# Router logits from rows less their mean, the inverse root applied behind the product, the last tile's comparisons on VectorE, and a pair's absorbed weights made inside the last tile's chain

## The chip, the cores and the metric

The kernel runs on one core of a Trainium2 chip. The metric is device time in microseconds (us) from launch to end on the slowest core, of which there is one here; lower is better. A kernel is timed in several runs and the median is taken. Names of engines: PE is the matmul engine (TensorE), DVE is VectorE, ACT is ScalarE, POOL is GpSimd and SP is SyncE, which issues most of the DMAs.

## The reference

The input x is 16 x 56 tokens of 256 numbers; a context of 16 x 1500 keys of 64 numbers stays the same in all layers. There are four layers of gated cross attention, each followed by a gated feed-forward part:

```python
x = x + jnp.tanh(g_xattn[l]) * attention_l(_layernorm(x, axis=-1), ctx_512, ...)
x = x + jnp.tanh(g_ffn[l])   * ffn_l(_layernorm(x, axis=-1), ...)
```

Layer 0 is plain attention with 16 heads and a mixture of 16 experts (the best 4 for each token) with a shared expert. Layers 1 to 3 are latent attention: a head's scores are a product of a turned query and the context, `scores = einsum('bhsr,bhlr->bhsl', q_r, k_r)`, a softmax over the keys, a weighted sum of the context and an output product. The feed-forward parts concerned here are those of layers 2 and 3:

```python
# layer 2: 8 experts, the best one
route = jax.nn.sigmoid(x @ router_w)
max_ind = jnp.argmax(route, axis=1)
# layer 3: 16 experts, the best four, weights divided by their sum
logits = jnp.einsum('bsh,eh->bse', x, router_w) + expert_bias
scores = jax.nn.softmax(logits, axis=-1)
top_w, top_idx = jax.lax.top_k(scores, TOP_K)
```

In both, x is the normalised row: `(x - m) / jnp.sqrt(v + eps)`. The factor 1/sqrt(v + eps) is one number for each row, so it can be applied to a row before the product with the router's weights, or to the row of logits behind it.

## The kernel before

**Tiles and stages.** x lies in the core's memory as 8 tiles of 112 tokens. The weights of latent attention are absorbed: for each of 8 pairs of heads, `absorbing` (L242 to L299) multiplies weights with weights in four stages, each some matmuls and one copy from PSUM: e (L274, L278), f (L282, L284), M (L291, L293) and G (L298, L299). `Next.absorb(...)` runs these stages for pairs of the layer that comes next. `queries(l)` (L314 on) makes all queries of the layer by pairs (L331, M times the normalised rows); pairs that are not ready yet are made inside it. Absorbed pairs that are ready come from the expert stage before.

**Attention.** `attention_mla` (L642 to L860) does 56 steps in a layer: 8 tiles by 7 groups of 128 query rows. The order on every engine is written out by hand: `in_order` pins each instruction in the order of the program text. The loop runs over k and works on three steps at once: step k gets its scores (L703) with the maxima of its first half (L715, L717), its exponentials (L726, L735), the maxima of its second half (L720) and `invert` (L746, L747: two sums of the denominators on POOL; L748: the reciprocal on DVE; L750: a transpose on DVE; then DMAs on SP that spread it). Step k-1 gets its probabilities turned (L765, with copies on DVE at L768 for two of the six groups and on ACT at L770 for four; the groups 1 to 3 go through the banks in which step k's first half had its scores). Step k-2 gets the product with the values (L777) and its scaling on DVE (L788).

**The router's chain.** After the last step of a tile, `project(t)` becomes the generator `after`: the output product (L800) and the addition to x (L802), then `router.token_tile(t)` (L921 to L1022). The loop advances it three yields a step:

```python
                next(after, None)
                if new:
                    new.exps0()
                    new.maxima1()
                next(after, None)
                next(after, None)
```

So the number of yields between two parts of `token_tile` sets how many steps apart they come, and the place of each on its engine's queue. The parts are: mean and variance (L928, L929); the inverse root, by shifts and three Newton rounds on DVE (L131 to L141, three yields behind the first round); the normalised row xr (L932); copies of xr for the four experts, two on ACT and one on POOL (L938), in layer 3 alone; transposes (L941) and their copy (L943); logits (L949); softmax or sigmoid (L954 to L971); comparisons of all pairs of experts (L977, L978 on DVE, L979, L980 on POOL); ranks (L984, L986); the counting product (L990, L992); places (L996 to L1010); and the scatter of each row to its experts' places in DRAM, an indirect DMA on POOL for each (L1013: four in layer 3, one in layer 2).

**The seam to the experts.** Behind the last step `attention_mla` drains `after` for the last tile. Then `moe` (L1165 on) makes the table of tiles (`r.table()`, L1117 on), runs `occupy(n)` (L115 to L119: n matmuls of ones in bf16 whose result nobody reads) and walks over tiles of 128 rows: row load (L1204), weight loads (L1197, L1198), transposes (L1211, L1213), gate and up products (L1223), activation (L1227, L1228), transposes of the hidden rows (L1234), down product (L1245) and the store of results (L1248). In layer 2 the absorbed pair 0 of layer 3 is made between `occupy` and the tiles, the pairs 1 and 2 behind them, and the weights of pair 2 are loaded when tile 3 is at work (L1306).

Of the kernel before, what the change touches and what calls it, by code (L numbers as in the profile page):

```python
# [41 lines left out]
ALU = mybir.AluOpType  # L42
# [3 lines left out]
B, S, D = 16, 56, 256  # L46
# [3 lines left out]
NT = B // 2  # L50
# [24 lines left out]
def flamingo_kernel(ctx: ExitStack, tc: tile.TileContext, d: dict, out: bass.AP):  # L75
    nc = tc.nc
# [38 lines left out]
    def occupy(n):  # L115

        ps = misc()
        for _ in range(n):
            in_order(nc.tensor.matmul(ps, onesb[:, 0:128], onesb, start=True, stop=True))  # L119
# [26 lines left out]
        return y  # L146

    def inverse_root_now(pool, var, n):
        root = inverse_root(pool, var, n)
        while True:  # L150
            try:
                next(root)
            except StopIteration as e:
                return e.value
# [37 lines left out]
    class Next:  # L192
# [11 lines left out]
        def absorb(self, *gs):  # L204

            todo = [absorbing(self.l, g, self.G, self.pool, self.made, in_order) for g in gs]
            while todo:
                todo = [a for a in todo if next(a, self) is not self]

        def tile(self, t):  # L210

# [24 lines left out]
    def load_absorbed(l, g):  # L236
        loaded[l, g] = [
            load_heads(n, d[f"L{l}_{n}"], g)
            for n in ("wqr", "wkr", "wkc", "wq", "wkv", "wo")
        ]  # L240
# [401 lines left out]
    def attention_mla(l, nxt, router=None, behind=None, tail=None):  # L642

        with ExitStack() as st:
# [173 lines left out]
            for k in range(n + 2):  # L818
# [30 lines left out]
                if val and val.j == nq - 1:  # L849
                    for _ in after:  # L850
                        pass
                    after = project(val.t)
            if tail is None:
                for _ in after:
                    pass
            else:

                next(after)
                next(after)
            return after  # L860


# [39 lines left out]
    class Router:  # L902
# [18 lines left out]
        def token_tile(self, t):  # L921
# [5 lines left out]
            mv = pool.tile([TP, 2], F32, name="mv")  # L927
            in_order(nc.vector.bn_stats(st, x[:, t, :]))  # L928
            in_order(nc.vector.bn_aggr(mv, st))  # L929
            rstd = yield from inverse_root(pool, mv[:, 1:2])  # L930
            xr = pool.tile([TP, top, DX], F32, name="xr")
            in_order(nc.vector.tensor_scalar(xr[:, 0, 0:D], x[:, t, :], mv[:, 0:1], rstd, ALU.subtract, ALU.mult))  # L932
            yield
            c = C_D4 + 4 * t if top == 4 else C_D1 + t
            in_order(nc.gpsimd.tensor_copy(xr[:, :, D : D + 1], small[0:TP, c : c + top].unsqueeze(2)))
            for j in range(1, top):
                copy = nc.gpsimd.tensor_copy if j == 3 else nc.scalar.copy
                in_order(copy(xr[:, j, 0:D], xr[:, 0, 0:D]))  # L938
            ps = misc()
            for k in range(2):  # L940
                in_order(nc.tensor.transpose(ps[:, k * TP : (k + 1) * TP], xr[:, 0, k * 128 : (k + 1) * 128], ident[0:TP, 0:TP]))  # L941
# [1 line left out]
            in_order(nc.scalar.copy(xt, ps[:, 0 : 2 * TP].rearrange("p (k c) -> p k c", k=2)))  # L943
            yield
            yield
            yield
            lg = misc()[0:TP, 0:n_e]
            for k in range(2):
                in_order(nc.tensor.matmul(lg, xt[:, k, :], self.wr[:, k, :], start=k == 0, stop=k == 1))  # L949
            p = pool.tile([TP, n_e], F32, name="p")  # L950
            red = pool.tile([TP, 2], F32, name="red")
            yield
            if l == 2:
                in_order(nc.vector.tensor_copy(p, lg))  # L954
            else:
                in_order(nc.vector.tensor_tensor(p, lg, self.bias, ALU.add))
                in_order(nc.vector.tensor_reduce(red[:, 0:1], p, AX.X, ALU.max, negate=True))
            yield
            yield
# [16 lines left out]
            rank = pool.tile([TP, n_e], F32, name="rank")  # L976
            in_order(nc.vector.tensor_tensor(eq, others, mine, ALU.is_equal))  # L977
            in_order(nc.vector.tensor_tensor(gt, others, mine, ALU.is_gt))  # L978
            in_order(nc.gpsimd.tensor_tensor(eq, eq, tri[:, 0:n_e, 0:n_e], ALU.mult))  # L979
            in_order(nc.gpsimd.tensor_tensor(gt, gt, eq, ALU.add))  # L980
            yield
            yield
            yield
# [178 lines left out]
            in_order(nc.sync.dma_start(rows[e * CT : (e + 1) * CT].rearrange("c p x -> p c x"), bcast(zero, 1, CT)))  # L1162
            yield

    def moe(r, nxt=None, tail=None, rest=None):  # L1165

        l = r.l
        n_e, ft, nf, top, n_t, n_sure = MOE[l]
# [2 lines left out]
        with ExitStack() as st:  # L1171
# [85 lines left out]
            if l == 0:  # L1257


                sh = Shared(pool, ps_h, ps_o, side)  # L1260
                now = [part for e in range(2) for part in sh.parts(e, 0)]
                between = [part for e in range(2) for part in sh.parts(e, 1)]
                before, last = tail
                next(last)
                now[0][0]()
                next(before)
                next(last)
                next(last)
                next(before)
                next(last)  # L1270
                next(last)
                now[1][0]()
                next(last)
                r.table()
                next(last)
                next(last)
                next(last)
            else:
                r.table()
            by_pe = {0: (0, 1, 3, 4, 5, 6), 2: (), 3: (0, 2, 4, 5, 6)}[l]  # L1280
            diag = {}
# [21 lines left out]

            def during(i):
                if l == 2 and i == 3:
                    load_absorbed(3, 2)  # L1306
                if i % 3 == 0 and rest:
                    next(rest, None)
                if i % 4 == 3 and between:
# [23 lines left out]
            else:  # L1333
                pd = pool("d", 1)
                r.finish_weights()
                occupy(14 if l == 3 else 8)
                if l == 2:
                    nxt.absorb(0)
            tiles(0, n_sure, weights, loads, during)
            for _ in rest or ():  # L1340
                pass
# [1 line left out]
            with tc.If(live > n_sure):  # L1343
                tiles(n_sure, n_t, [], [])
            if nxt:
                nxt.absorb(*((0, 1) if l == 0 else (1, 2)))
            right.close()
            pt = pool("t", NT, **side)
            back = []
# [213 lines left out]
        for _ in left:  # L1563
            pass
    with routed(2) as r:
        attention_mla(2, nxt, r)
        nxt.whole.close()
        nxt = Next(3)
        moe(r, nxt)
    with routed(3) as r:  # L1570
        attention_mla(3, nxt, r)
        nxt.whole.close()
        moe(r)

# [142 lines left out]
```

## Time and profile before

| | us |
|---|---|
| median of 3 runs | 2395.82 |
| the runs | 2396.52, 2392.44, 2395.82 |
| profiled execution, its own time | 2395.73 |
| its span | 2393.6 |

The span runs from the first to the last instruction; what lies around it is 2.1 us. The clock that PE was granted is 0.964 of full speed over the span.

| engine | busy us | share of the span |
|---|---|---|
| PE | 2244.0 | 94% |
| DVE | 1531.0 | 64% |
| ACT | 1231.9 | 51% |
| POOL | 411.6 | 17% |

Where the groups of the table of costs are shown, a line reads: line of the kernel, engine, operation, output and inputs with their shapes, and the count, then busy time, the mean of one in nanoseconds, and the idle time of that engine just before them with what ended most of it. Two lines for the parts that the steps of attention are made of:

```profile
L703 PE MATMUL s_ps<-kvT,qT 64*128 64x500 f32 x2016 | 485.0, 608 | 11.2 <-ACT p L735 4.6
L777 PE MATMUL m_ps<-pT,kv 125*64 125x128 f32 x8064 | 477.3, 275 | 1.8 <-ACT pT L770 1.2
```

A timeline line gives the start in us from the span's start, the length, the engine, the line and the operation; in brackets stands how long the engine was idle before it and what released it. In the list of waits a line says who waited for whom, then the total in us, how many times, and the longest.

The stretches that matter are layer 2's attention (its first score group behind the first projection of that layer at 1249.16, and its last work near 1565), the seam behind it (the expert loop's first gate product at 1585.22), layer 3's queries (from about 1655), layer 3's attention (to about 2224) and the seam behind that (first gate product at 2244.53).

### The profile page before, as it was taken

The numbers are of one execution on the slowest core, as the hardware profiler recorded it, in microseconds if no ns is written. First come the engines' busy times: TensorE is split into PE (matmuls) and PEld (weight loads), VectorE is DVE, ScalarE is ACT, GpSimd is POOL, SyncE is SP. The second block draws the span as 40 slices with busy tenths as digits, with TensorE's granted clock in tenths as the row PEclk, the third lists the DMA queues.
The fourth block names the chain that finished last, engine by engine and source line by source line (L and its number), as shares of the span: only waits on it lengthen the run. The fifth ranks groups of instructions, "written<-read, shape, count | busy, mean of one in ns | idle before, by whom it ended". The sixth has DMA issues, their size and how long they took to land. (4 is left out here: it accounts for less than half of the span.)

```text
span 2393.6 us, 47915 instructions
## 1 busy us (share of the span) xinstructions
PE 2244.0 (94%) x17842; PEld 1611.7 (67%) x17842; DVE 1531.0 (64%) x3552; ACT 1231.9 (51%) x2703; POOL 411.6 (17%) x707
## 2 busy tenths in 40 slices
PE   8678989999999999999999999979899999999697
PEld 5445655777777776447777777745577777777454
DVE  5752245778777777667777777724577777776222
ACT  4312336666666663346666666513566666665131
POOL 5454710000000002420000000001001111111233
PEclk9769989999999999989999999999899999999899
DMA  7726752000000002100000000054101000000597
GB/s 226 217 87 190 228 140 81 22 21 22 21 21 22 21 23 69 54 28 21 24 24 11 23 22 23 11 209 148 34 22 30 29 20 26 26 26 18 158 285 205
DMA packets 116676, 172.98 MB, mean 72 GB/s; under 512 B 20154, under 2 KB 78531, under 8 KB 115412
## 3 DMA queue, kind: packets, MB, share of 16 engines
q1 hardware_dynamic: 106902, 151.35, 20.6%
q0 software_dynamic: 7600, 17.14, 2.2%
q8 instruction: 144, 2.36, 0.4%
q10 hardware_dynamic: 1934, 1.34, 0.2%
q14 instruction: 96, 0.79, 0.1%
HBM read 131.24 MB, written 40.48 MB: 72 GB/s over the span
## 5 line engine op out<-in xcount | busy, mean ns | idle before, releaser
L726 ACT ACTIVATE p<-s_ps,nm 128x500 f32<-128x500 f32 x504 | 335.7, 675 | 362.7 <-DVE nm L717 362.7
L703 PE MATMUL s_ps<-kvT,qT 64*128 64x500 f32 x2016 | 485.0, 608 | 11.2 <-ACT p L735 4.6
L777 PEld LDWEIGHTS m_ps<-pT,kv 125*64 125x64 f32 x8064 | 436.7, 137 | 65.8 <-issue 57.1
L777 PE MATMUL m_ps<-pT,kv 125*64 125x128 f32 x8064 | 477.3, 275 | 1.8 <-ACT pT L770 1.2
L715 DVE TENSOR_REDUCE part<-s_ps 128x1 f32<-128x500 f32 x504 | 340.3, 677 | 214.6 <-PE s_ps L703 214.0
L703 PEld LDWEIGHTS s_ps<-kvT,qT 64*128 64x128 f32 x2016 | 186.5, 189 | 196.6 <-issue 122.7
L765 PE MATMUL m_ps<-ident,p 128*125 128x128 f32 x2016 | 297.9, 283 | 0.3
L720 DVE TENSOR_REDUCE nm<-s_ps 128x1 f32<-128x1500 f32 x168 | 287.2, 1709 | 1.9 <-PE s_ps L703 1.9
L765 PEld LDWEIGHTS m_ps<-ident,p 128*125 128x125 f32 x2016 | 248.0, 188 | 36.1 <-issue 26.6
L735 ACT ACTIVATE p<-s_ps,nm 128x1500 f32<-128x1500 f32 x168 | 254.9, 1517 | 0.8 <-DVE nm L720 0.8
L765 PE MATMUL s_ps<-ident,p 128*125 128x128 f32 x2016 | 249.5, 274 | 0.0
L746 POOL TENSOR_TENSOR den<-den 128x1 f32<-128x1 f32 x168 | 32.9, 196 | 1215.0 <-ACT p L726 1214.8
L765 PEld LDWEIGHTS s_ps<-ident,p 128*125 128x125 f32 x2016 | 234.8, 189 | 0.5
L770 ACT COPY pT<-s_ps 125x512 f32<-125x512 f32 x336 | 181.0, 596 | 99.0 <-PE s_ps L765 83.2
L770 ACT COPY pT<-m_ps 125x512 f32<-125x512 f32 x336 | 185.2, 618 | 0.0
L1223 PE MATMUL gu_ps<-wgu,xT 128*128 128x448 f32 (+2 forms) x344 | 142.9, 543 | 21.3 <-DMA wgu<-in_L_wgu 14.2
L788 DVE TENSOR_TENSOR ctxT<-m_ps,rep 64x128 f32<-64x128 f32 (+1 forms) x384 | 104.4, 272 | 89.7 <-PE m_ps L777 79.3
L1228 DVE TENSOR_TENSOR act<-gu_ps,act 128x224 f32<-128x224 f32 (+2 forms) x78 | 31.2, 401 | 187.9 <-ACT act L1227 173.5
L768 DVE COPY pT<-m_ps 125x512 f32<-125x512 f32 x168 | 116.2, 691 | 10.0 <-PE s_ps L765 0.9
L312 ACT COPY qT<-q_ps 64x224 f32<-64x224 f32 x128 | 71.8, 561 | 97.5 <-PE q_ps L356 60.3
L768 DVE COPY pT<-s_ps 125x512 f32<-125x512 f32 x168 | 114.3, 680 | 0.0
L1223 PEld LDWEIGHTS gu_ps<-wgu,xT 128*128 128x128 f32 x344 | 63.2, 194 | 72.5 <-issue 30.6
(293 smaller groups left out, 2604.6 us busy)
## 6 DMA issues: line engine op xcount, KB each, us to landing
wgu<-in_L_wgu SPq DMA_DIRECT2D x36, 448.0 KB
rows<-zero SPq DMA_DIRECT2D x16, 899.5 KB
kvT<-turned_kv SPq DMA_DIRECT2D x16, 750.0 KB
wgu<-in_L_wgu SPq DMA_DIRECT2D x34, 352.0 KB
rep<-through SPq DMA_DIRECT2D x336, 32.0 KB
xrow<-rows SPq DMA_DIRECT2D x78, 128.5 KB
wgu<-in_L_wgu SPq DMA_DIRECT2D x8, 1024.0 KB
wd<-in_L_wd SPq DMA_DIRECT2D x36, 224.0 KB
```

Of the source, the lines that this page charges most:

```text
L312: nc.scalar.copy(o, i)
L703: in_order(nc.tensor.matmul(o[:, 0 : 4 * KP], qT[64 * b : 64 * b + 64, t, j * QT : (j + 1) * QT], kvTs[t][64 * b : 64 * b + 64, z * 4 * KP ...
L715: in_order(nc.vector.tensor_reduce(self.part[:, z : z + 1], sp0[z][:, 0 : 4 * KP], AX.X, ALU.max))
L720: in_order(nc.vector.tensor_reduce(self.nm[1], sp1[:, :, 0 : 4 * KP], AX.XY, ALU.max, negate=True))
L726: in_order(nc.scalar.activation(self.p[0][:, 4 * z * KP : 4 * (z + 1) * KP], sp0[z][:, 0 : 4 * KP], AF.Exp, bias=self.nm[0], accum_out=sel ...
L735: in_order(nc.scalar.activation(self.p[1].rearrange("p (z c) -> p z c", z=3), sp1[:, :, 0 : 4 * KP], AF.Exp, bias=self.nm[1], accum_out=se ...
L765: in_order(nc.tensor.transpose(ps[:, c, :], self.p[b][:, k : k + KP], ident))
L768: in_order(nc.vector.tensor_copy(o, ps))
L770: in_order(nc.scalar.copy(o, ps))
L777: in_order(nc.tensor.matmul(self.pv[64 * b : 64 * b + 64, :], kv[:, self.t, c, b, :], self.pT[:, c, b, :], start=c == 0, stop=c == KC - 1))
L788: in_order(nc.vector.tensor_tensor(ctxs[self.t][64 * a : 64 * a + 64, b, lo - 448 * a : hi - 448 * a], self.pv[64 * b : 64 * b + 64, cols] ...
L1223: in_order(nc.tensor.matmul(ps[:, s, 0:n], xT[:, k, :], wgu[:, k, s * n : (s + 1) * n], start=k == 0, stop=k == 1))
```

## The change

It has five parts.

- `token_tile` subtracts the mean only (L932). Transposes and logits are taken from that; the root's second part runs two yields behind the transposes, in one go with no yields inside (`rest_of`), and multiplies xr on DVE; the copies for the experts stand behind the logits; the logits are multiplied with the root when they are read (L954, L956). The generator has three yields fewer between the mean and the transposes, and the same number from there on.
- For the last tile alone, the two comparisons of L979 and L980 are DVE's.
- For layers 2 and 3 `attention_mla` no longer drains the last tile's generator; it advances it by two yields and returns it. `moe` drains it. In layer 2 it runs the four stages of layer 3's pair 0 in between, one stage behind each of the first groups of yields (2, 2, 1, 1). The rest of the generator follows, then the loads of pair 2's weights, then the table.
- In layer 2, pair 1 takes the place of pair 0 between `occupy` and the tiles, pairs 2 and 3 that of 1 and 2 behind them, and the loads at tile 3 are those of pair 3. Layer 3's queries then find four pairs ready.
- In layer 3, `occupy` runs 26 matmuls in place of 14.

```diff
--- before.py
+++ after.py
@@ -146,7 +146,9 @@
         return y
 
     def inverse_root_now(pool, var, n):
-        root = inverse_root(pool, var, n)
+        return rest_of(inverse_root(pool, var, n))
+
+    def rest_of(root):
         while True:
             try:
                 next(root)
@@ -206,6 +208,9 @@
             todo = [absorbing(self.l, g, self.G, self.pool, self.made, in_order) for g in gs]
             while todo:
                 todo = [a for a in todo if next(a, self) is not self]
+
+        def stages(self, g):
+            return absorbing(self.l, g, self.G, self.pool, self.made, in_order)
 
         def tile(self, t):
 
@@ -850,13 +855,9 @@
                     for _ in after:
                         pass
                     after = project(val.t)
-            if tail is None:
-                for _ in after:
-                    pass
-            else:
-
-                next(after)
-                next(after)
+
+            next(after)
+            next(after)
             return after
 
 
@@ -927,15 +928,14 @@
             mv = pool.tile([TP, 2], F32, name="mv")
             in_order(nc.vector.bn_stats(st, x[:, t, :]))
             in_order(nc.vector.bn_aggr(mv, st))
-            rstd = yield from inverse_root(pool, mv[:, 1:2])
+
             xr = pool.tile([TP, top, DX], F32, name="xr")
-            in_order(nc.vector.tensor_scalar(xr[:, 0, 0:D], x[:, t, :], mv[:, 0:1], rstd, ALU.subtract, ALU.mult))
+            in_order(nc.vector.tensor_scalar(xr[:, 0, 0:D], x[:, t, :], mv[:, 0:1], None, ALU.subtract))
+            root = inverse_root(pool, mv[:, 1:2])
+            next(root)
             yield
             c = C_D4 + 4 * t if top == 4 else C_D1 + t
             in_order(nc.gpsimd.tensor_copy(xr[:, :, D : D + 1], small[0:TP, c : c + top].unsqueeze(2)))
-            for j in range(1, top):
-                copy = nc.gpsimd.tensor_copy if j == 3 else nc.scalar.copy
-                in_order(copy(xr[:, j, 0:D], xr[:, 0, 0:D]))
             ps = misc()
             for k in range(2):
                 in_order(nc.tensor.transpose(ps[:, k * TP : (k + 1) * TP], xr[:, 0, k * 128 : (k + 1) * 128], ident[0:TP, 0:TP]))
@@ -943,17 +943,22 @@
             in_order(nc.scalar.copy(xt, ps[:, 0 : 2 * TP].rearrange("p (k c) -> p k c", k=2)))
             yield
             yield
+            rstd = rest_of(root)
+            in_order(nc.vector.tensor_scalar(xr[:, 0, 0:D], xr[:, 0, 0:D], rstd, None, ALU.mult))
             yield
             lg = misc()[0:TP, 0:n_e]
             for k in range(2):
                 in_order(nc.tensor.matmul(lg, xt[:, k, :], self.wr[:, k, :], start=k == 0, stop=k == 1))
+            for j in range(1, top):
+                copy = nc.gpsimd.tensor_copy if j == 3 else nc.scalar.copy
+                in_order(copy(xr[:, j, 0:D], xr[:, 0, 0:D]))
             p = pool.tile([TP, n_e], F32, name="p")
             red = pool.tile([TP, 2], F32, name="red")
             yield
             if l == 2:
-                in_order(nc.vector.tensor_copy(p, lg))
+                in_order(nc.vector.tensor_scalar(p, lg, rstd, None, ALU.mult))
             else:
-                in_order(nc.vector.tensor_tensor(p, lg, self.bias, ALU.add))
+                in_order(nc.vector.scalar_tensor_tensor(p, lg, rstd, self.bias, ALU.mult, ALU.add))
                 in_order(nc.vector.tensor_reduce(red[:, 0:1], p, AX.X, ALU.max, negate=True))
             yield
             yield
@@ -976,8 +981,10 @@
             rank = pool.tile([TP, n_e], F32, name="rank")
             in_order(nc.vector.tensor_tensor(eq, others, mine, ALU.is_equal))
             in_order(nc.vector.tensor_tensor(gt, others, mine, ALU.is_gt))
-            in_order(nc.gpsimd.tensor_tensor(eq, eq, tri[:, 0:n_e, 0:n_e], ALU.mult))
-            in_order(nc.gpsimd.tensor_tensor(gt, gt, eq, ALU.add))
+
+            engine = nc.vector if t == NT - 1 else nc.gpsimd
+            in_order(engine.tensor_tensor(eq, eq, tri[:, 0:n_e, 0:n_e], ALU.mult))
+            in_order(engine.tensor_tensor(gt, gt, eq, ALU.add))
             yield
             yield
             yield
@@ -1162,7 +1169,7 @@
             in_order(nc.sync.dma_start(rows[e * CT : (e + 1) * CT].rearrange("c p x -> p c x"), bcast(zero, 1, CT)))
             yield
 
-    def moe(r, nxt=None, tail=None, rest=None):
+    def moe(r, nxt=None, tail=None, rest=None, left=None):
 
         l = r.l
         n_e, ft, nf, top, n_t, n_sure = MOE[l]
@@ -1276,6 +1283,16 @@
                 next(last)
                 next(last)
             else:
+
+                stages = nxt.stages(0) if nxt else iter(())
+                for n in (2, 2, 1, 1):
+                    for _ in range(n):
+                        next(left)
+                    next(stages, None)
+                for _ in left:
+                    pass
+                if nxt:
+                    load_absorbed(3, 2)
                 r.table()
             by_pe = {0: (0, 1, 3, 4, 5, 6), 2: (), 3: (0, 2, 4, 5, 6)}[l]
             diag = {}
@@ -1303,7 +1320,7 @@
 
             def during(i):
                 if l == 2 and i == 3:
-                    load_absorbed(3, 2)
+                    load_absorbed(3, 3)
                 if i % 3 == 0 and rest:
                     next(rest, None)
                 if i % 4 == 3 and between:
@@ -1333,9 +1350,9 @@
             else:
                 pd = pool("d", 1)
                 r.finish_weights()
-                occupy(14 if l == 3 else 8)
+                occupy(26 if l == 3 else 8)
                 if l == 2:
-                    nxt.absorb(0)
+                    nxt.absorb(1)
             tiles(0, n_sure, weights, loads, during)
             for _ in rest or ():
                 pass
@@ -1343,7 +1360,7 @@
             with tc.If(live > n_sure):
                 tiles(n_sure, n_t, [], [])
             if nxt:
-                nxt.absorb(*((0, 1) if l == 0 else (1, 2)))
+                nxt.absorb(*((0, 1) if l == 0 else (2, 3)))
             right.close()
             pt = pool("t", NT, **side)
             back = []
@@ -1563,14 +1580,14 @@
         for _ in left:
             pass
     with routed(2) as r:
-        attention_mla(2, nxt, r)
+        left = attention_mla(2, nxt, r)
         nxt.whole.close()
         nxt = Next(3)
-        moe(r, nxt)
+        moe(r, nxt, left=left)
     with routed(3) as r:
-        attention_mla(3, nxt, r)
+        left = attention_mla(3, nxt, r)
         nxt.whole.close()
-        moe(r)
+        moe(r, left=left)
```

## The prediction

> **What bounds the kernel now.** I read the page first, then the timeline of TensorE (PE) from one score group to the next in layers 2 and 3, then the list of waits for what lies between, then the timelines of the two places where attention gives way to the experts.
>
> ```profile
> PE 2244.0 (94%) x17842; PEld 1611.7 (67%) x17842; DVE 1531.0 (64%) x3552; ACT 1231.9 (51%) x2703; POOL 411.6 (17%) x707
> ```
>
> PE is busy 94% of the span, so an edit on another engine counts only where PE waits for it. The change touches layers 2 and 3 of attention and what follows them. There a step of attention begins with the score matmuls (L703); the columns are start, duration, engine and line:
>
> ```profile
> 1838.78 2.79 PE L703 MATMUL s_ps<-kvT,qT 64*128 64x500 f32 x12
> 1841.50 3.82 PE L800 MATMUL m_ps<-G,ctxT 128*112 128x256 f32 x16
> ...
> 1859.42 2.79 PE L703 MATMUL s_ps<-kvT,qT 64*128 64x500 f32 x12
> 1862.14 0.41 PE L941 MATMUL m_ps<-ident,xr 112*128 112x112 f32 x2
> ...
> 1868.06 2.79 PE L703 MATMUL s_ps<-kvT,qT 64*128 64x500 f32 x12
> ```
>
> Start to start, the seven steps of this layer 3 tile last 12.06 (it holds the projection, L800), 8.58, 8.64 (router transposes L941), 8.80 (logits L949), 8.50, 8.30 and 8.80 us (ranks L990, L992). A step without router work lasts 8.30. In the 8.58 step VectorE (DVE) is late instead: the rest of the inverse root and the normalising lie ahead of its copies of turned weights (L768), and the next scores start 0.09 us behind the second copy. One more wait stands beside these, in six tiles of layer 3:
>
> ```profile
> DVE wide L748 <- POOL den L746: 12.7, 4, 3.2
> ...
> DVE wide L748 <- issue: 6.4, 2, 3.2
> ```
>
> ```profile
> 1840.47 0.94 POOL L1013 DMA_INDIRECT rows<-xr,sloti  x1 [0.30 <-issue]
> ...
> 1841.94 0.17 DVE L748 RECIPROCAL wide<-den 128x2 f32<-128x2 f32 x1 [3.24 <-issue]
> ...
> 1842.27 1.81 DVE L715 TENSOR_REDUCE part<-s_ps 128x1 f32<-128x500 f32 x3
> 1844.11 0.16 DVE L717 TENSOR_REDUCE nm<-part 128x1 f32<-128x3 f32 x1
> 1844.19 1.71 DVE L720 TENSOR_REDUCE nm<-s_ps 128x1 f32<-128x1500 f32 x1
> ```
>
> GpSimd (POOL) issues the four scatters of a tile's rows from 1836.65 to 1841.41; its additions of denominators (L746) stand behind them, DVE's reciprocal waits for those, and the maxima wait behind the reciprocal. Today nobody pays: PE does the 3.82 us projection meanwhile.
>
> **The Trainium skill.** "TensorE: Matmul & The Clock Gate", section on the array of sixteen 32x32 tiles, says that ScalarE (ACT) and VectorE run strictly in order, so one late operand holds everything queued behind. The trace agrees: maxima at 1842.27 although the scores started at 1838.78. The same page, "What's actually happening": after an idle window (3.4 us) the array runs at half clock. The trace agrees in the second seam below. "GPSIMD Engine Reference", section 3.1, has a tensor_tensor on GpSimd near half the speed of VectorE; here 0.84 and 0.72 us for 112x256 against 0.42. "DMA: Bandwidth & Descriptors", SWDGE path, says that a GpSimd DMA costs about 2 us, mostly receipt; here the last scatter's issue ends at 2237.42 and the load that needs it issues at 2241.43, 4.0 us.
>
> **Part A, logits from x less its mean.** DVE gains a subtraction (about the 0.41 us of L932) in the projection's step, hidden: its second copy would end about 11.8 us after the step's start, the next scores start at 12.06. Everything behind moves ahead three yields, which is one step. The 8.58 and 8.64 steps merge into one of 8.65 and a plain 8.30. Saved 8.58 + 8.64 - 8.65 - 8.30 = 0.27, say 0.28 with layer 2's 8.59, in 7 tiles of 2 layers: -3.9. The later multiplication (0.41 on DVE) and the row copies moved behind the logits fall into steps whose PE work is longer (8.80) or have that slack. Bounds 0 and -5.
>
> **Part B, the scatter loses its cover.** One step earlier, the scatter's wait falls into the step before the projection, a plain 8.30. In the step shown the second maximum (L720) ends at 1845.90, 7.12 after the scores started (5.3 in steps without the wait). Behind it stand the merge L788 and two copies, 0.61 + 0.69 + 0.68 = 1.98, so the second copy ends at 9.1 and the next scores start at 9.2: 0.9 over 8.30, six tiles, +5.4. Bounds: 0 if it stays covered, 6 x 3.24 = 19.4 if the whole wait reaches PE. Layer 2 has one scatter a tile and no such wait.
>
> **Part C, layer 3's queries.** Four pairs of heads are ready instead of three. A pair made inside the queries costs 5.87 us there (L274 at 1674.22, 1680.08, 1685.95), a ready one 2.34 per half (L331 at 1657.30, 1659.64, 1661.98), 4.68 a pair: -1.2. Bounds: -0.5, and -2.8, the pair's PE work at the layer 2 seam (0.66 + 0.49 + 1.0 + 0.65).
>
> **Part D, seam of layer 2.** Last tile's transposes stood at 1568.10 behind the root; they move ahead about 2.1. But four stages of a pair of layer 3 are threaded in, and ACT's exponential (1569.79) comes behind their copies e, M and G (0.27, 0.37, 0.37 in the trace): near 1571.0, +1.2; comparisons on DVE give back 0.26. The table is some 0.95 later, and the experts, PE-bound at 5.8 a tile, start that much later: +0.95 (0.6 to 1.2). The pair made after the table stays there, as another pair. The moved weight load on SP's queue (six issues) is done before the first expert weights at 1577.67.
>
> **Part E, seam of layer 3.**
>
> ```profile
> 2226.31 0.31 ACT L963 ACTIVATE p<-p,red 112x16 f32<-112x16 f32 x1 [1.43 <-DVE red L957]
> ...
> 2227.72 0.84 POOL L979 TENSOR_TENSOR eq<-eq,tri 112x256 f32<-112x256 f32 x1 [3.36 <-DVE eq L977]
> ...
> 2229.39 0.42 DVE L984 TENSOR_REDUCE rank<-gt 112x16 f32<-112x256 f32 x1 [1.42 <-POOL gt L980]
> ```
>
> No stages here. The exponential comes at about 2225.1 (two row copies, 0.71 on ACT, now stand ahead of it and eat part of the root's 2 us); the two comparisons take 0.84 on DVE in place of 1.56 and two hand-overs on POOL. Rank at 2227.6 in place of 2229.39: -1.8 (1.6 to 2.0). It passes through slots and scatters to the first expert tile's rows.
>
> **Part F, 26 dummy matmuls for 14.** The 14 took 4.39 (half of them at 0.43, the others 0.2); 26 take about 6.9 and end before the rows land.
>
> ```profile
> 2235.86 4.39 PE L119 MATMUL m_ps<-onesb 128*128 128x512 bf16 x14
> ...
> 2244.53 2.79 PE L1223 MATMUL gu_ps<-wgu,xT 128*128 128x448 f32 x4 [0.46 <-ACT xT L1213]
> ...
> 2248.39 3.35 PE L1223 MATMUL gu_ps<-wgu,xT 128*128 128x448 f32 x4 [0.46 <-ACT xT L1213]
> ...
> 2252.82 1.77 PE L1223 MATMUL gu_ps<-wgu,xT 128*128 128x448 f32 x4 [0.46 <-ACT xT L1213]
> ```
>
> ```profile
> 2246.00:2251.00 5.00, 4.54 (x8) 1.66 (x7) 0.51 (x2) 0.73 (x2) 0.00 (x0) 0.50 1.01 315
> ```
>
> The clock column reads 0.50, and the first two tiles take 2.79 and 3.35 where the third takes 1.77. With PE warm 2.6 us of matmul go, but the DMA share is 1.01 there, and the second tile's rows landed at 2247.1, so tile 2 can start only about 1.7 earlier. Taken -1.7 (0 to -3).
>
> **Part G.** In the drain of layer 3 one merge (L788) waited 3.4 us for what the profile calls remote; layer 2's same place has no such wait. About 1.7 us of it look like chance, of which I count half: -0.8 (0 to -1.7).
>
> **Sum.** -3.9 + 5.4 - 1.2 + 0.95 - 1.8 - 1.7 - 0.8 = -3.05. Against the profiled execution's own 2395.73 that is 2392.7; the median of the runs, 2395.82, is 0.1 away. I use 0.2% (4.8 us) as what a measurement here can tell from no change.
>
> **Rivals.** *R1, the scatter stays covered*: B is 0 because DVE catches up in slack behind it. For it: in a plain step DVE works about 6.3 of 8.30 us. Against: the 9.1 just worked out. -8.45: 2387.3. *R2, the expert stream swallows E and F*: DMA share 1.01 at 2246 to 2251 says that weights, not rows, may set the next start. Against: the share is 0.52 just behind. -3.05 + 3.5: 2396.2. *R3, slower*: B's wait of 3.24 reaches PE whole, since exponentials and turned copies on ACT slip with the maxima. It decides from B above 1.41 us a tile (slower than before at all), and 2.2 (by 0.2%). Whole: -8.45 + 19.4 = +11: 2406.7. Against it: a step without the wait leaves DVE room, as the 7.12 shows.
>
> **Numbers.** Forecast 0.50, R1 0.28, R2 0.12, R3 0.10. The range, 2386.0 to 2398.5, takes in R1 but its low tail and R2, and leaves out R3: about 2 in 10 outside. Faster by over 0.2% (below 2391.0): 0.35 of the forecast, nearly all of R1: 0.46. Slower: R3 and a little: 0.12. Within: 0.42.
>
> **What would show it.** A: the step with L941 directly behind the projection's, at 8.65. B: L748 waiting 3.2 in the step before the projection, and that step near 9.2; 8.3 speaks for R1, over 10 for R3. C: one of the 5.87 spacings gone. D: table about 1 us later after the last attention. E, F: rank 1.8 earlier, the first two expert tiles at 1.75. I am wrong above all if B is.

## The result: 0.19% slower, where 0.13% faster was forecast

| | before | changed |
|---|---|---|
| median of 22 runs each, us | 2397.32 | 2402.77 |
| profiled execution, us | 2395.73 | 2405.67 |
| its span, us | 2393.6 | 2403.9 |

The ratio of the changed kernel to the one before is 1.0019, with a 95% interval of 1.0010 to 1.0028. A second set of 22 runs on another occasion gave 1.0021 (1.0012 to 1.0031). By the ratios the change costs 4 to 5 us (the medians differ by 5.4); the median is outside the range of 2386.0 to 2398.5 that the prediction gave.

The busy times on the page of the changed kernel explain nothing: PE is 94% busy as before, DVE 64%, ACT 51%.

The two spans differ by 10.3 us, twice what the medians differ by. So the span was cut at landmarks read off the timelines, in both kernels and in x8, a second profile of the changed kernel (us of each stretch; a score group is the matmuls of one step's scores, the table is taken from its first matmul, and layer 2's first score group stands at 1045.2 before, the 1249.16 named earlier being the step of its third projection):

| stretch | before | changed | x8 |
|---|---|---|---|
| start to the scores of layer 1 | 386.8 | 392.1 | 385.2 |
| to the scores of layer 2 | 658.4 | 660.4 | 657.9 |
| layer 2, first to last score group | 498.1 | 496.5 | 496.3 |
| last projection to table | 13.8 | 15.8 | 15.7 |
| table to first gate product | 10.9 | 12.8 | 10.8 |
| first to last gate product | 42.1 | 44.3 | 41.9 |
| last gate product to layer 3's scores (the queries) | 69.4 | 65.2 | 65.1 |
| layer 3, first to last score group | 500.7 | 501.9 | 502.4 |
| last score group to last projection (the drain) | 18.9 | 21.4 | 21.8 |
| last projection to table | 16.4 | 14.3 | 14.3 |
| table to the fourth tile's gate product | 23.0 | 23.4 | 22.1 |
| to the end | 137.9 | 138.8 | 137.7 |

The first two stretches hold no changed instruction, and they account for 7.3 of the 10.3 us: in x8 they are 2.1 shorter than before instead. Two profiles can't be compared by their spans here; the stretches, and the length of single steps, can. Five rows are alike in both profiles of the changed kernel and away from before: layer 2 (-1.7), the table of layer 2 (+1.9), the queries (-4.2, part of it a half-clock stretch from 1637.6 to 1644.4 that the profile of before has there), the drain of layer 3 (+2.5 to +2.9) and the chain behind it (-2.1). x3 has such a stretch in its queries, too (67.9), so it comes and goes. Layer 3's row hides its steps, since in before some of the first ones ran at half clock.

**The steps of layer 3.** In the changed kernel a tile has the steps 8.64, 8.80, 8.70, 8.30, 8.80, 9.11 and 12.05 us, together 64.40 where it was 63.67. The 8.58 is gone, as forecast. The step before the projection is this one (timeline of the changed kernel, from one score group to the next):

```profile
1898.90 2.79 PE L708 MATMUL s_ps<-kvT,qT 64*128 64x500 f32 x12
...
1900.48 0.93 POOL L1020 DMA_INDIRECT rows<-xr,sloti  x1 [0.30 <-issue]
...
1901.94 0.17 DVE L753 RECIPROCAL wide<-den 128x2 f32<-128x2 f32 x1 [3.16 <-issue]
...
1904.19 1.71 DVE L725 TENSOR_REDUCE nm<-s_ps 128x1 f32<-128x1500 f32 x1
...
1907.18 0.68 DVE L773 COPY pT<-s_ps 125x512 f32<-125x512 f32 x1
...
1908.01 2.79 PE L708 MATMUL s_ps<-kvT,qT 64*128 64x500 f32 x12
...
1910.73 3.82 PE L805 MATMUL m_ps<-G,ctxT 128*112 128x256 f32 x16
```

The wait of 3.16 us is the old one, one step earlier: DVE's reciprocal waits for sums that stand behind the four scatters on POOL. The second maximum ends 7.00 after the scores started, the second copy at 8.96, the next scores start at 9.11. The projection comes in the step after, where it hides nothing. The other longer step, 8.70 for 8.50, was not forecast:

```profile
1873.10 2.79 PE L708 MATMUL s_ps<-kvT,qT 64*128 64x500 f32 x12
...
1879.13 0.42 DVE L983 TENSOR_TENSOR gt<-p 112x256 f32<-112x256 f32 x1
...
1879.47 0.92 DVE L793 TENSOR_TENSOR ctxT<-m_ps,rep 64x64 f32<-64x64 f32 x4
...
1881.03 0.68 DVE L773 COPY pT<-s_ps 125x512 f32<-125x512 f32 x1
...
1881.80 2.79 PE L708 MATMUL s_ps<-kvT,qT 64*128 64x500 f32 x12
```

Once in a tile the merge L793 (L788 before) writes four pieces and takes 0.92 in place of 0.61, since the 128 query rows of that step lie across the border at 448. Before, this fell in the step of the logits, whose PE work is longer; now the comparisons (L982, L983) stand ahead of it in the same step, and DVE's copies end 0.2 later.

**The drain of layer 3.** The drain is what attention does behind its last score group. The waits of the changed kernel show the scatter's wait in all its places, and one wait that had been 3.4:

```profile
DVE wide L753 <- issue: 19.1, 6, 3.2
...
DVE ctxT L793 <- remote: 5.7, 1, 5.7
```

```profile
2216.81 1.47 PE L770 MATMUL s_ps<-ident,p 128*125 128x128 f32 x12
...
2218.34 0.94 POOL L1020 DMA_INDIRECT rows<-xr,sloti  x1 [0.30 <-issue]
2220.36 0.61 DVE L793 TENSOR_TENSOR ctxT<-m_ps,rep 64x128 f32<-64x128 f32 x2 [5.68 <-remote]
2220.58 1.07 ACT L775 COPY pT<-s_ps 125x512 f32<-125x512 f32 x2 [7.47 <-issue]
```

PE's records go on to 2218.3, but DVE and ACT, which both wait for PE, stand still and start again together at 2220.4, when POOL's fourth scatter (issued until 2219.28) is over. Among the semaphore events of the trace (the signs by which one engine tells another that an instruction is done), the five that PE owed by then arrive between 2220.33 and 2220.57, the first of them 4.0 us behind the end of its matmul. These ends are modelled, so whether the matmuls or only their events were late can't be told. x8 has the same picture (first event 4.1 late, 1.2 after the last issue). Before, the same wait lay one step later and was shorter (timeline of before; the event came at 2215.52 for a matmul that ends at 2213.80):

```profile
2214.55 0.94 POOL L1013 DMA_INDIRECT rows<-xr,sloti  x1 [0.30 <-issue]
2215.55 0.61 DVE L788 TENSOR_TENSOR ctxT<-m_ps,rep 64x128 f32<-64x128 f32 x2 [3.42 <-remote]
2215.79 0.93 POOL L1013 DMA_INDIRECT rows<-xr,sloti  x1 [0.30 <-issue]
```

**The seam of layer 3.** The chain of the last tile is as forecast:

```profile
2235.87 0.30 ACT L968 ACTIVATE p<-p,red 112x16 f32<-112x16 f32 x1
...
2238.35 0.42 DVE L991 TENSOR_REDUCE rank<-gt 112x16 f32<-112x256 f32 x1
```

Rank comes 10.98 us after the start of the last projection (2227.37), where it was 13.09 (2216.30 to 2229.39). But it passes to the rows otherwise than forecast. POOL's second scatter follows the first after 3.3 us where it followed after 1.6, so the last scatter is issued 20.3 after the projection's start, and before it was 20.2. The first gate product still comes 26.7 after the projection's start in place of 28.2, because the load of the first rows follows the end of the last issue after 2.45 us (2248.58 to 2251.03; 2.26 in x8) and not after 4.0; why isn't shown. The dummies bring little:

```profile
2254.08 1.77 PE L1230 MATMUL gu_ps<-wgu,xT 128*128 128x448 f32 x4 [0.46 <-ACT xT L1220]
2257.23 0.41 PE L1218 MATMUL m_ps<-ident,xrow 128*128 128x128 f32 x2 [1.38 <-DMA xrow<-rows]
2258.10 2.74 PE L1230 MATMUL gu_ps<-wgu,xT 128*128 128x448 f32 x4 [0.46 <-ACT xT L1220]
```

The first tile's products take 1.77 instead of 2.79. Then PE waits 1.38 for the second tile's rows, and here the second tile's products run at half clock again (2.74). That last part is this profile's own: in x8, the same program, they take 1.77. The wait for the second rows is there, too (1.58).

**The seam of layer 2.** The timeline of the changed kernel, then two of its windows; behind the five engines' busy times stand the granted clock, the DMA share and GB/s:

```profile
1574.26 1.97 PE L296 MATMUL m_ps<-f,wq 128*128 128x64 f32 x8
...
1577.33 0.37 ACT L304 COPY G<-m_ps 128x256 f32<-128x256 f32 x1 [0.69 <-PE m_ps L303]
1577.59 0.21 ACT L966 ACTIVATE p<-p 112x8 f32<-112x8 f32 x1
...
1594.69 6.32 PE L1230 MATMUL gu_ps<-wgu,xT 128*128 128x512 f32 x8 [0.46 <-ACT xT L1220]
```

```profile
1583.00:1590.00 7.00, 5.85 (x26) 2.94 (x26) 1.13 (x6) 0.27 (x1) 0.12 (x1) 0.50 0.64 220
1590.00:1597.00 7.00, 6.16 (x18) 3.55 (x18) 0.51 (x2) 2.40 (x4) 0.00 (x0) 0.50 1.04 423
```

The exponential L966 stands behind the pair's last copy, as forecast, but the pair's matmuls run at half clock (1.97 where the trace before has 1.10), and PE stays there until 1600.0 though it is busy 84 and 88% in these windows. The first gate products take 6.32 where they took 3.70. In x8, the same program, they take 3.70.

### The profile page after: what moved, and what is told of

It is laid out like the page before. It is cut to its first block, busy times and chain, and to the rows that moved or that the text cites. A ratio compares the mean times of both kernels' runs of the same rounds, so it can differ in the third digit from the quotient of the medians.

```text
span 2403.9 us, 47956 instructions
## 1 busy us (share of the span) xinstructions
PE 2254.7 (94%) x17849; PEld 1616.4 (67%) x17854; DVE 1536.2 (64%) x3572; ACT 1232.3 (51%) x2703; POOL 408.8 (17%) x703
## 5 line engine op out<-in xcount | busy, mean ns | idle before, releaser
L793 DVE TENSOR_TENSOR ctxT<-m_ps,rep 64x128 f32<-64x128 f32 (+1 forms) x384 | 104.3, 272 | 84.8 <-PE m_ps L782 72.1
L773 DVE COPY pT<-m_ps 125x512 f32<-125x512 f32 x168 | 116.2, 692 | 10.3 <-PE s_ps L770 0.9
```

Of the source, the lines that this page charges most:

```text
L773: in_order(nc.vector.tensor_copy(o, ps))
L793: in_order(nc.vector.tensor_tensor(ctxs[self.t][64 * a : 64 * a + 64, b, lo - 448 * a : hi - 448 * a], self.pv[64 * b : 64 * b + 64, cols] ...
```

## The experiments

Ratios are to the kernel before on the same chip, with 95% intervals. x1 to x4 ran on one chip, x5 to x8 on a second, x9 to x12 on a third. The changed kernel has 1.0019, and 1.0021 (x8) beside x5 to x7; beside the others it was not timed, so there it can be compared only across chips.

**x1, x6: the chain a step later.** In x1:

```diff
             yield
             yield
+            if t < NT - 1:
+                yield
+                yield
+                yield
             rstd = rest_of(root)
```

> The changed kernel with three more yields between the transposes and the rest of the root, for all tiles but the last, so that everything from the rest of the root on comes one step later while mean, subtraction and transposes stay early. Theory 1 (the scatter without cover and the comparisons in the step of the four-piece merge): the layer 3 steps of 9.11 and 8.70 go back to 8.30 and 8.50, a tile lasts 63.4 instead of 64.40, six tiles give -6.0 against the changed kernel; the scatter of tile 6 falls one step later in the drain, whose last score group to last projection goes from 21.4 to 17 to 19. Ratio to the kernel before 0.997 to 0.9995. Rival 1 (steps of the tiles matter little, the difference lies in half-clock windows at the seams): tile period shorter but the time stays 3 to 5 us over the kernel before, ratio 1.001 to 1.002.

Measured: 0.9986 (0.9975 to 0.9997). x2, x3 and x4, on the same chip and with the long steps, have 1.0006 to 1.0010. So theory 1 holds and rival 1 falls: the step lengths of layer 3 do set the time. The drain fell to 19.7 only, not to the 17 to 19 expected, and the tile lasted 63.61 and not 63.4. The 9.11 and the 8.70 went (8.30, 8.50), while the root's rest, now alone in its step, makes that one 8.52: what the change wins by merging two steps it wins only while the root's rest is hidden behind the longer step of the logits. In x6 the three yields stand behind the exponential:

> The changed kernel with three more yields behind the exponential, for all tiles but the last: comparisons and scatter one step later, while the root's rest stays in the step of the logits, whose PE work is longer. (With the yields ahead of the root's rest that step grew from 8.30 to 8.52.) Theory 1: layer 3 steps 12.05, 8.64, 8.80, 8.30, 8.50, 8.30, 8.80, together 63.4, against 64.40 in the changed kernel and 63.67 before; layer 2 keeps 63.18; six tiles give -6.0 against the changed kernel. Ratio to the kernel before 0.9975 to 0.9995.

Measured: 0.9981 (0.9972 to 0.9991), on the chip where the changed kernel had 1.0021; the intervals lie apart. Steps 12.05, 8.64, 8.80, 8.30, 8.50, 8.30 and 8.80: 63.39 a tile. Here is where the scatter falls (timeline of x6): the wait is as long as ever, and PE projects through it.

```profile
1902.67 3.82 PE L805 MATMUL m_ps<-G,ctxT 128*112 128x256 f32 x16
...
1902.98 0.17 DVE L753 RECIPROCAL wide<-den 128x2 f32<-128x2 f32 x1 [3.16 <-issue]
```

The drain is 18.9, as before. But behind the wait the last projection takes 5.47 at half clock, where before and the changed kernel have 3.79, and last projection to table is 16.0 (in x1, too).

**x12: the scatter alone later.** The same three yields just ahead of the slot numbers (`is_j = ...`, ahead of L1014).

> The changed kernel with three more yields just ahead of the places and the scatter, for all tiles but the last: the scatter one step later, the comparisons where the change put them. Theory 1 (two separate costs): layer 3 steps 12.05, 8.64, 8.80, 8.70, 8.30, 8.80 or 8.30, 8.30 to 8.80: the 9.11 goes, the 8.70 stays, the tile lasts 63.6. Rival 6 (the 8.70 is an echo of the late scatter, too): both go, 63.4.

One profiled execution, no ratio: steps 8.64, 8.80, 8.70, 8.30, 8.80, 8.60 and 12.05, 63.89 a tile where 63.6 was expected. The 8.70 stays, so it is a cost of its own, and rival 6 falls. The 9.11 became 8.60, not 8.30. The likely reason is that the operations that make the slot numbers (L1014 to L1028 of the changed kernel, 1.3 us on DVE) moved into that step with the scatter and stand ahead of its copies.

**x5, x9: the drain.** Tile 6's scatters are put off into the last tile's chain; what they read (`xr`, `sloti`, in x9 `slot` too) gets a second buffer. In x9:

```diff
+            if l == 3 and t == NT - 1:
+                self.held()
             p = pool.tile([TP, n_e], F32, name="p")
...
-            in_order(nc.vector.tensor_copy(sloti, slot))
-            flat = rows.rearrange("a p c -> (a p) c")
-            for j in range(top):
+            def scatter():
+                in_order(nc.vector.tensor_copy(sloti, slot))
+                flat = rows.rearrange("a p c -> (a p) c")
+                for j in range(top):
...
+            if l == 3 and t == NT - 2:
+                self.held = scatter
+            else:
+                scatter()
```

> The changed kernel, but the four scatters of layer 3's tile 6 are held back and issued in the last tile's chain, right behind its logits, where DVE and ACT work for some 5 us without PE; xr and the slot numbers of layer 3 get a second buffer for it. Theory 1 (PE's semaphores arrive late while POOL issues four scatters, and this is what lengthened the drain): last score group to last projection in layer 3 falls from 21.4 to about 17.2, as in layer 2; the chain behind it stays within 0.5 of 14.3 (projection to table); 3 to 5 us off the changed kernel. Rival 5 (the wait named remote in the drain is the spread of the denominators by DMA, or chance): the drain stays above 20.

x5, where the cast of the slot numbers stayed in its old place, gave 1.0011 (1.0000 to 1.0023), and only one of the four scatters left the drain: the program's order of POOL took the other three early. The drain fell to 18.6, and DVE's merge went on at 2215.05, 0.9 after the third scatter's issue, as it had gone on 1.1 after the fourth. That fits theory 1 but isn't the test that was meant. x9 is:

> As x5, but with the cast of tile 6's slot numbers moved with its scatters into the last tile's chain, so that all four of them leave the drain (in x5 only the last did; three stayed, and the drain was 18.6). Theory 1 (PE's semaphores come late while POOL issues scatters): no wait of DVE's merge above 3.1 in the drain, last score group to last projection 17.2 as in layer 2, PE not at half clock there; the time from the last projection to the table stays 14.3. Rival 5 (something else in the drain, the spread of the denominators or chance): 18.5 or more remains.

Measured: 0.9992 (0.9980 to 1.0003), below the changed kernel's intervals, though those are from other chips. The drain is 17.18, like that of layer 2 (17.17 in before), no wait named remote is left there, and the chain behind it lasts 14.34, as in the changed kernel (14.28). With no scatter in the drain, PE's events there come within 0.03 us of the modelled ends. The last merge still waits for its product, longer than the 3.1 expected as the most (4.07; 4.33 in the changed kernel). From the timeline of x9:

```profile
2214.13 0.61 DVE L793 TENSOR_TENSOR ctxT<-m_ps,rep 64x128 f32<-64x128 f32 x2 [1.91 <-PE m_ps L782]
...
2220.17 0.61 DVE L793 TENSOR_TENSOR ctxT<-m_ps,rep 64x128 f32<-64x128 f32 x2 [4.07 <-PE m_ps L782]
...
2220.93 3.79 PE L805 MATMUL m_ps<-G,ctxT 128*112 128x256 f32 x16 [0.81 <-DVE ctxT L793]
```

So the four scatters in the drain make the wait, and the second buffers don't take it away: x5 has them, too, and with three scatters left its merge waits 4.24. Rival 5 falls: the spread of the denominators is the same in x9. The wait that before had in its drain was no chance either: its drain is 1.7 over layer 2's, and its late event was 1.7 late.

**x2: the pair out of the last tile's chain.**

```diff
-                stages = nxt.stages(0) if nxt else iter(())
+                stages = iter(())
...
-                if nxt:
-                    load_absorbed(3, 2)
...
-                    nxt.absorb(1)
+                    nxt.absorb(0)
```

> The changed kernel with the pair's four stages taken out of the last tile's chain again: pair 0 is made after the table, pairs 1 and 2 behind the tiles, weights of pair 2 loaded at tile 3; the rest is as changed. Theory 1 (the stages delay the last tile's exponential on ScalarE, and with it the table, and leave PE at half clock when the first expert tile comes): last projection to table in layer 2 falls from 15.75 to about 11.4, the first gate product comes some 4 us earlier, and layer 3's queries are longer by 1.2 (one pair more inside them) to 4; time 0 to 3 below the changed kernel, ratio 1.0005 to 1.002. Rival 2 (a pair ready before the queries is worth more than the delay): 1 to 4 us above the changed kernel, ratio 1.002 to 1.0035.

Measured: 1.0009 (0.9998 to 1.0019). Last projection to table fell from 15.8 to 12.2, and the queries grew from 65.2 to 66.5: a pair made ahead is worth 1.3 and costs 3.5 where it was put. By the intervals x2 can't be told from the changed kernel, but the two stretches can.

**x3, x11: 16 dummies in layer 2** (`occupy(26 if l == 3 else 16)`).

> The changed kernel with 16 dummy matmuls in place of 8 in layer 2. Theory 1 (8 matmuls of 0.43 fill one window of the clock only by luck; in the changed kernel's profile PE stayed at half clock from 1572.7 to 1600.0): the first gate products of layer 2 take 3.7 instead of 6.3, the absorbed stages before them half as long; 1 to 4 us below the changed kernel, ratio 0.9998 to 1.0015. Rival 3 (the first rows set the start and the clock recovers anyway): no change within 1 us, ratio 1.0015 to 1.0025.

Measured: 1.0010 (1.0000 to 1.0020). First to last gate product took 41.7; over all profiles this stretch has two values, 41.7 to 42.1 where the clock was up when the first tile came, and 44.3 to 45.4 where it wasn't. With 8 dummies it was up in before and in four of the eleven profiles of the changed kernel and its variants (x2, x4, x8, x12) and down in seven; with 16 it was up in both profiles. In time this wasn't shown, here or in x11 below.

**x4: 14 dummies in layer 3**, as before.

> The changed kernel with 14 dummy matmuls in place of 26 in layer 3. Theory 1 (26 keep the clock up for the first expert tile, as the prediction had it): first gate to fourth tile's gate grows from 11.0, the first tile's products 2.8 instead of 1.77, time 0.5 to 2 above the changed kernel. Rival 4 (the second tile's rows and the weights' stream set the fourth tile's start): first gate to fourth tile's gate stays 11 to 11.3, time unchanged within 0.5.

Measured: 1.0006 (0.9997 to 1.0015), with the changed kernel's interval, from other chips, overlapping. The first tile's products take 3.35; with 26 they take 1.77 in eleven of twelve profiles, so the clock part of theory 1 holds. Its time part doesn't: first gate to the fourth tile's gate was 10.4 with 14, and 9.4 to 11.6 with 26. Table to the fourth tile's gate product was 23.0 with 14 (in before, too), and between 21.7 and 24.0 with 26 (mean 22.5 of twelve profiles). So rival 4 holds in the main: 12 more dummies bring about 0.5 us, an estimate from one profile with 14 in this program and one of before.

**x8: the changed kernel once more.**

> The changed kernel once more, for a second profile of the same program and for a comparison on the same chip. Theory 1: the tile steps of layer 3 (8.64, 8.80, 8.70, 8.30, 8.80, 9.11, 12.05) and the drain (21.4) are the same to 0.5, since they follow from order; what stands before layer 1 and the half-clock windows at the seams differ by several us. Ratio to the kernel before 1.0005 to 1.0025.

Measured: 1.0021 (1.0012 to 1.0031), with steps and drain as expected. Its own profiled execution took only 2390.22, which shows how little one execution says.

**x7, x10, x11: the edits together.** x7 is x6 with the edits of x2 and x5; x10 takes x9's in place of x5's; x11 is x10 with 16 dummies in layer 2.

> Three edits together on the changed kernel: comparisons and scatter a step later, the pair's stages out of the last tile's chain, tile 6's scatters held back. If the costs found so far are separate they add up: -6.0 for the tiles, -3 for the drain, -2 for the seam of layer 2, together 9 to 12 below the changed kernel and 4 to 8 below the kernel before, ratio 0.9965 to 0.9985. If the gain in the drain is only handed on to the wait for the first rows, 0.998 to 0.9995.

x7: 0.9969 (0.9959 to 0.9980), within what adding up gave. The drain is 18.8 and the projection behind it ran at half clock, as in x6.

> As x7 with the cast held too. If theory 1 holds in the drain: last score group to last projection 17.2 in place of 18.8 and no half clock in the projection, 2 to 4 below x7, ratio to the kernel before 0.9955 to 0.998. If the eight scatters in a row now hold the first rows up, the gain is handed on: 0.9965 to 0.9985.

x10: 0.9951 (0.9934 to 0.9968), median 2384.63 where before had 2394.35: faster than the kernel before, and below the changed kernel's intervals. The drain is 17.18, the projection behind it takes 3.79, and layer 3's table to first gate product is 12.23, no longer than with four scatters in the row (12.25 in x8); nothing was handed on.

> As x10 with 16 dummy matmuls in layer 2 in place of 8. Theory 1 (8 dummies fill a window of the clock only when they happen to lie right): layer 2's table to first gate about 11.8, its gates 41.7 in place of up to 45, whatever the position of the windows; 0 to 3 below x10 on the mean. Rival 3: no difference.

x11: 0.9963 (0.9944 to 0.9982), not apart from x10. Its gates took 41.9 in place of 44.6, but table to first gate 13.1 in place of 12.8 (11.8 was expected); a net gain from gate products at full clock could not be shown in time.

## Why the prediction was wrong, by its steps

- **A, steps merged: right.** -0.28 a tile, as layer 2 shows undisturbed (63.47 to 63.18). x1 adds the condition: the root's rest must lie in a step with room.
- **B, the scatter's cover: right.** 0.9 a tile forecast, 9.11 - 8.30 = 0.81 measured; six tiles +4.9. R1 (it stays covered) and R3 (the whole 3.24 reaches PE) are both out.
- **Left out: the collision of the comparisons with the four-piece merge**, 0.20 in six tiles, +1.2. Part A moved "everything behind one step ahead" and priced the multiplication and the row copies in their new steps, but not the comparisons. The merge's second form stood in the timeline.
- **C, queries: right.** -1.2 forecast, -1.3 between x2 and the changed kernel. The rest of the 4.2 in the table goes with the half-clock stretch in the one profile of before.
- **D, seam of layer 2: right in kind, too small.** +0.95 forecast; the table is +1.9 later in the changed kernel and x8 (+0.7 to +1.9 over the profiles with the pair in the chain). The term that was off is the pair's matmuls, priced at their duration at full clock. In x1 and x3 the pair ran at full clock and the table is +0.9 and +0.7 later, as forecast; in the other seven profiles with the pair there, part of it ran at half clock. Where the clock then stays down, gate products cost another 2 to 4.
- **E, last tile's chain: right up to the table.** -1.8 forecast, -2.1 measured. What it says behind that, that the gain passes through the scatters, isn't what happened: the last scatter was issued no earlier, and the first gate product came 1.5 earlier because the load of the rows followed the last issue sooner.
- **F, dummies: wrong.** -1.7 forecast, about -0.5 measured. The price came from the first two tiles' matmuls, and they did get shorter; but the second tile was to start about 1.7 earlier, and it did not: its gate products start 16.1 to 16.9 behind the table in the twelve profiles with 26, 16.9 in x4 and 15.7 in before. With 26, PE waits for its rows in eleven of the twelve (1.2 to 1.8). The 26 themselves took 7.1 to 8.5 us, not 6.9, and ended only as the first rows came. R2 was half right: F was swallowed, E was not.
- **G, the drain: wrong, and of the wrong sign.** This is the step that failed most: 3.5 of the 6.5 us between the forecast and the sum below. The wait named remote was taken "like chance", and half of it counted as a gain of 0.8. It belongs to the four scatters (x9); the change moved them a step ahead in the drain as everywhere, and the drain grew by 2.5 to 2.9. Part B asked what the scatter meets in a tile of the loop, and nowhere what it meets behind the last one.

With the measured sizes the steady terms add up to: A -3.4 (over the six tiles whose steps all lie in the loop), B +4.9, collision +1.2, C -1.3, D +1.9, E -2.1, F -0.5, G +2.7, together +3.4. The first three make +2.7; all steps behind the first tile, added up in the two profiles, give -2.0 in layer 2 and +4.6 in layer 3, so +2.6. The runs show +4.6, with 2.4 to 6.7 as its interval, so the sum fits. A rest, if there is one, may be the half clock in the seam of layer 2, which was there in seven of eleven profiles; how often it was there before isn't known, since there is one profile of that kernel.

## What to carry to other kernels

Where instructions are placed by counting steps, a part made shorter moves everything behind it, so each moved instruction has to be priced in its new step, in the loop and again in the drain, where less work covers it. A wait that the profile can't name is not chance until a second profile or a second place shows it missing; ask what else runs at that time. Compare profiles stretch by stretch: here 7 of 10 us between two spans lay in code that had not changed.

## What the runs showed that was not expected

- In the drain, while POOL issues four indirect DMAs in a row (1.24 us from one to the next), events of PE reach DVE and ACT up to 4.1 us behind the modelled ends, and come in a burst near the end of the row (1.1 after the last issue in the changed kernel, between the third and the fourth in before). With the scatters elsewhere the wait is gone (drain 17.18 in place of 21.4). But a row of scatters alone is not enough: in the loop of the changed kernel, with the row at 1896.71 to 1901.41, the five events of PE from 1896.80 to 1898.55 come within 0.02 us of the ends, and in the last tile's chain of x9 the held scatters cost nothing (14.34 for 14.28). What the drain adds, and by what path the scatters hold PE's events up, isn't shown.
- PE can be busy 84 to 88% of a window at half clock and stay there (1583 to 1597), until 1600.0, 5.3 us into gate products that run without a gap. In the clock records of these traces half-clock stretches last multiples of 3.41 us (in the seam of layer 2: 10.24 before, 27.31 in the changed kernel, 13.65 in x8; the last of a trace is cut off by its end), and 8 dummies of 0.43 us are about as long as one such unit.
